# Gathers listed 20 chunks ahead, and steps of six turns whose last adds run in the next step, in a graph layer on one core

## The chip, the cores and the metric

The kernel runs on one core of one Trainium2 chip. Its time is the device time of one execution in microseconds (us). The kernel before took 1976.42 us, the median of three runs (1966.72, 1976.42 and 1977.36).

## The reference

One layer of a message-passing network with residual and layer norm. There are N = 12500 nodes with 128 features each and E = 400000 edges, sorted by their destination `dst`; `src` and the type (0 or 1) of an edge are random. All matrices are 128 x 128.

```python
msg = where(edge_type == 0, x[src] @ W_data.T + b_data, x[src] @ W_ctrl.T + b_ctrl)
agg = segment_sum(msg, dst, num_segments=12500)
out = layernorm(x + relu(agg + x @ W_self.T + b_self))      # over the 128 features, no scale, no shift
```

Since the sum over edges is linear, the kernel sums the rows `x[src]` for each node and type first (and counts the edges for the biases), and multiplies by the weights after. So most of the work is fetching 400000 rows of x by index and adding them up by destination.

## The kernel before

**Data.** x is split at the start into three bf16 parts whose sum is the float32 value (`split_x`, lines 229 to 269). The parts are kept in SBUF as `x3` and stored to DRAM as the table `rows3`, 768 bytes a row. Splitting uses ScalarE (lines 246 and 248) and VectorE (247 and 249); x arrives in eight pieces through ScalarE's DMA queue (line 241), at most four of them in SBUF at a time, and `store` (253) writes the table through SP's queue.

**Two ways to fetch a row.** The edges lie in 3125 chunks of 128, and these in 25 groups of 125. A group is cut into four windows, and each window into a "p" part of 12, 11, 11 or 11 chunks and an "e" part of 20 chunks. So there are 100 windows ("pairs" in the code).

* A **p** chunk is gathered: GpSimd issues one indirect DMA (line 700) that brings 128 rows of `rows3` into a tile `msg`. TensorE multiplies the three parts with a 0/1 matrix `psel` (line 658, three matmuls) that adds each row to the column of its destination, and a fourth matmul with `one_col` counts (712). There are 1125 such chunks.
* An **e** part is fetched from SBUF by TensorE. VectorE sorts its 2560 edges into slots, by the block of x that they read (`give_slots`, lines 505 to 637): 100 blocks, 32 slots each. A matrix `pick` of zeros and ones then selects rows of `x3` (line 732, 98 matmuls, "picks", each 32 x 384, four beside one another in the array) into the PSUM tile `got`. ScalarE copies `got`, two groups of rows at a time, to `emsg` in SBUF (line 743), and TensorE adds the rows up by destination with `esel` (658; VectorE makes `esel` from the slots' codes in three selections, line 463) and counts (761). Edges that find no slot, up to 64 a window, are "spares": their rows come by one more indirect DMA into `last` (line 747).

**A step.** The main loop takes one window w per step (`picked`, lines 718 to 797). The window's 25 groups of rows q are worked on in turns of four: turn t = 0 to 5 picks the rows q = 4t to 4t+3 (`rows`), counts and adds those of the turn before, and a seventh unit, t = 6, adds the last ones, turns the codes and calls `accumulate`, which adds the PSUM tile `sums` into the SBUF accumulator `acc` (line 688). `got` has two buffers in PSUM, `sums` two (shared by the p and the e part), the tile `rk` one.

Beside the picks of w, a step does these things for other windows: the p chunks of a window two steps back (`gathered`, 690 to 716, spread over steps by the lines after `chunks, closed, rest`); the slots of w+2 in the order `before` (TensorE, lines 537 and 479), `ranks` and `rank_matrix` (VectorE, 547 to 562 and 589, the latter makes `rv`), `put` (TensorE, 601, 20 matmuls into `rk`), `spread` (ScalarE copies `cell`, two DMAs on SP's queue write it to DRAM and read it back to all partitions as `pick`), and `turn_codes` and `keep_codes` (TensorE 621 and 489, ScalarE 631, 496 and 498, VectorE 500); the comparison that makes `pick` of w+1 a 0/1 matrix (643); the first selections for w+3; the preparation of the next group's indices and codes (`prep_e`, `prep_p`); and the finishing of 500 nodes (`finish`: product with the weights, norm, store).

**What sets the order.** `merged` sorts the units of all these lists by a position between 0 and 1 within the step, which gives the order in which the program lists instructions. The framework's scheduler then orders each engine's queue from that list: an instruction listed later may be put ahead of one that, by the scheduler's own estimate, isn't ready yet. Each engine runs its queue strictly in that order; buffers of a pool come round in turn, and an instruction waits for the earlier user of its buffer. The pool `msg` has 24 buffers (`AHEAD`). In the queue of GpSimd as built, a spare-row gather therefore stands between chunk gathers whose use comes some two steps later.

**The first part.** Before the loop: loads of indices (`load_first`, `load`, `near_i`, SP's queue), constants, the weights and biases through ScalarE's queue (274 and 275), the places of all windows (`place`, `near`) and the transposed weights `wT`, then the slots of windows 0 and 1 mixed with the splitting of x, then `bparts` (small DMAs of the biases), `store_rows` and `prep_p(0)`.

A long path at the end of the program (a plain loop over all chunks) runs only if a check finds that the input doesn't fit the windows; it isn't taken here.

## Time and profile before

| | us |
|---|---|
| median of three runs | 1976.42 |
| the profiled execution | 2371.03 |
| its span, first to last instruction | 2369.3 |
| TensorE busy / weight loads busy | 1863.1 / 1364.9 |
| VectorE, ScalarE, GpSimd busy | 1584.0, 1229.7, 1412.5 |
| mean granted TensorE clock | 0.909 of full speed |

The profiled execution is longer than the timed ones; only shares and single durations are taken from it, and the times compared are those of the runs. In the profile, PE is TensorE, PEld its weight loads, DVE VectorE, ACT ScalarE, POOL GpSimd and SP the engine whose queue issues most plain DMAs. A row such as "POOL msg L700 <- PE sums L658" means that the instruction of line 700 on GpSimd that writes `msg` waited for an instruction of TensorE, line 658; the numbers are the total in us, how often, and the longest. In a timeline row the first two numbers are start and duration in us, and the bracket at its end is the idle time before it and what ended it. "issue" is a wait for which the profile shows nothing. The busy share of an engine is a mean over the whole span, so the waits and the order of work around a step's boundary say more than the shares.

### The profile page before, as it was taken

How to read it: one execution, taken by the hardware profiler on the slowest of the kernel's cores; microseconds unless marked ns; L12 is line 12 of the kernel's file. 1: busy time of each engine (PE TensorE's matmuls, PEld its weight loads, DVE VectorE, ACT ScalarE, POOL GpSimd, SP SyncE). 2: the span in 40 equal slices, each digit the busy share in tenths (PEclk: the TensorE clock that was granted, in tenths of full speed). 3: DMA queues.
4: the chain of work that ended last, by engine and by line, in shares of the span. 5: the costliest groups of instructions: out<-in, count | busy, mean ns of one | idle time of the engine just before them, and what ended most of it. 6: DMA issues, size and time to landing. Idle time of an engine off the chain costs nothing.

```text
span 2369.3 us, 70786 instructions
## 1 busy us (share of the span) xinstructions
PE 1863.1 (79%) x28867; PEld 1364.9 (58%) x28867; DVE 1584.0 (67%) x4224; ACT 1229.7 (52%) x2322; POOL 1412.5 (60%) x1243
## 2 busy tenths in 40 slices
PE   0468887887878787888888887888888888887977
PEld 0346665665556565666565565665666665665646
DVE  6747676766666666767676766676667666676753
ACT  3435554555445545545555554555555555545635
POOL 0366665756465565665666665566666665676661
PEclk9879898999889899999999988998989999999979
DMA  7423342333333333333323323333323323233321
GB/s 206 148 80 104 97 107 84 109 91 98 87 96 96 100 100 90 109 97 94 108 85 106 107 86 102 97 98 106 107 83 104 102 88 102 89 101 105 97 87 42
DMA packets 185017, 236.73 MB, mean 100 GB/s; under 512 B 80295, under 2 KB 152282, under 8 KB 184682
## 3 DMA queue, kind: packets, MB, share of 16 engines
q0 software_dynamic: 57200, 115.59, 17.7%
q1 hardware_dynamic: 114418, 109.94, 14.8%
q10 hardware_dynamic: 13064, 6.60, 1.0%
q8 instruction: 228, 3.74, 0.7%
q14 instruction: 107, 0.88, 0.1%
HBM read 215.35 MB, written 16.64 MB: 98 GB/s over the span
## 4 chain that ended last, share of the span: by engine, by line
PE 66%; issue 10%; ACT 10%; DVE 6%; another core or an unknown queue 5%; DMA 1%; SPq 1%; DVEq 0%; ACTq 0%; POOL 0%; POOLq 0%
PE sums L658 32%; PE got L732 22%; ACT emsg L743 9%; PE fin L850 3%; PE rk L601 2%; PE sums L761 2%; PE rk L489 1%; PE sums L712 1%; DVE esel L463 1%; PE rk L537 1%; DVE x L249 1%; PE rk L621 1%; DVE xt L247 0%; PE fin L837 0%
## 5 line engine op out<-in xcount | busy, mean ns | idle before, releaser
L700 POOL DMA_INDIRECT msg<-rows,pidx x1125 | 1290.4, 1147 | 790.3 <-PE sums L658 363.4
L743 ACT CAST emsg<-got 128x768 bf16<-128x768 f32 x1200 | 919.8, 804 | 796.5 <-PE got L732 328.8
L732 PE MATMUL got<-x,pick 128*32 128x384 bf16 x9800 | 659.2, 353 | 238.7 <-ACT emsg L743 145.6
L658 PE MATMUL sums<-esel,emsg 128*128 128x176 bf16 x7200 | 751.3, 255 | 48.6 <-issue 46.0
L658 PEld LDWEIGHTS <-emsg 128*128 128x128 bf16 x7200 | 579.8, 104 | 220.0 <-issue 215.4
L463 DVE TENSOR_TENSOR esel<-code_col,code 128x1408 bf16<-128x1408 bf16 (+1 forms) x300 | 275.0, 917 | 348.9 <-PE sums L658 195.7
L732 PEld LDWEIGHTS <-pick 128*32 128x32 bf16 x9800 | 242.3, 97 | 421.3 <-issue 336.0
L658 PE MATMUL sums<-psel,msg 128*128 128x48 bf16 x3375 | 240.0, 187 | 48.0 <-issue 35.3
L658 PEld LDWEIGHTS <-msg 128*128 128x128 bf16 x3375 | 187.8, 99 | 77.6 <-issue 72.5
L747 POOL DMA_INDIRECT last<-rows,idx x100 | 118.1, 1181 | 139.4 <-DMA pdst<-in_dst_dram 91.4
L712 PE MATMUL sums<-psel,one_col 128*128 128x48 bf16 x1125 | 184.5, 185 | 16.9 <-issue 16.8
L688 DVE TENSOR_TENSOR acc<-acc,sums 128x352 f32 (+1 forms) x200 | 94.0, 470 | 132.5 <-PE sums L658 54.0
L761 PE MATMUL sums<-esel,one_col 128*32 128x176 bf16 x2500 | 168.2, 254 | 16.2 <-issue 14.7
L463 DVE TENSOR_TENSOR O<-cell_col,blk 128x2000 bf16<-128x2000 bf16 x100 | 119.3, 1193 | 55.7 <-PE got L732 27.8
L643 DVE TENSOR_SCALAR pick<-pick,lane_f 128x1600 bf16<-128x1600 bf16 x200 | 125.6, 642 | 14.2 <-DMA pick<-there 13.7
L601 PE MATMUL rk<-rv,O 128*128 128x64 bf16 x2000 | 89.0, 198 | 50.3 <-DVE rv L589 35.0
L761 PEld LDWEIGHTS <-one_col 128*32 128x32 bf16 x2500 | 84.2, 103 | 63.7 <-issue 31.1
L547 DVE TENSOR_REDUCE ahead<-rk 128x100 bf16<-128x500 f32 x100 | 67.5, 675 | 78.7 <-PE got L732 55.7
L712 PEld LDWEIGHTS <-one_col 128*128 128x128 bf16 x1125 | 109.6, 97 | 18.0 <-issue 17.7
L551 DVE TENSOR_TENSOR prod<-O,ahead 128x2000 bf16<-128x2000 bf16 x100 | 119.0, 1190 | 0.0
L601 PEld LDWEIGHTS <-O 128*128 128x128 bf16 x2000 | 73.4, 101 | 67.3 <-issue 54.8
L631 ACT CAST code<-rk 128x50 bf16<-128x50 f32 x100 | 20.3, 203 | 173.8 <-PE got L732 68.0
(170 smaller groups left out, 1998.4 us busy)
## 6 DMA issues: line engine op xcount, KB each, us to landing
pick<-there SPq DMA_DIRECT2D x100, 800.0 KB
msg<-rows,pidx POOLq DMA_INDIRECT x1125
rows<-x SPq DMA_DIRECT2D x6, 1344.0 KB
xs<-in_x_dram SPq DMA_DIRECT2D x99, 62.5 KB
out_dram<-h SPq DMA_DIRECT2D x99, 62.5 KB
xt<-in_x_dram ACTq DMA_DIRECT2D x6, 896.0 KB
psrc<-in_src_dram SPq DMA_DIRECT2D x100, 6.0 KB
pdst<-in_dst_dram SPq DMA_DIRECT2D x100, 6.0 KB
```

The costliest lines, as they stand in the source:

```text
L463: nc.vector.tensor_tensor(sel.rearrange("p n (w t) -> p n w t", t=2), col[:rows].rearrange("p (o w t) -> p o w t", o=1, t=2).to_broadcast( ...
L551: nc.vector.tensor_tensor(prod, s["O"], ahead.rearrange("p (o j) -> p o j", o=1).to_broadcast([P, EC, NCELL]), op=OP.mult)
L601: nc.tensor.matmul(s["rk"][:m, :2 * CAP], s["held"][:, c * NCELL:c * NCELL + m], s["rv"][:, c].rearrange("p v r -> p (v r)"), start=(c == ...
L643: nc.vector.tensor_scalar(t, t, lane_f, None, op0=OP.is_equal)
L658: nc.tensor.matmul(out, msg[:, j * D:(j + 1) * D], sel, start=(start and j == 0), stop=stop, skip_group_check=True)
L688: added.append(nc.vector.tensor_add(win, win, ps[:, :4 * wide].rearrange("p (a w) -> p a w", w=wide)[:, :, :width]))
L700: nc.gpsimd.indirect_dma_start(out=msg, out_offset=None, in_=rows3[:, :], in_offset=bass.IndirectOffsetOnAxis(ap=codes["p", g][0][:, i * P ...
L712: nc.tensor.matmul(cnt, one_col, sel, start=False, stop=(c == n - 1), skip_group_check=True)
L732: nc.tensor.matmul(ps[CAP * a:CAP * (a + 1), :], slots[w]["pick"][:, a * NQ + q, :], x3[:, 4 * q + a - a0].rearrange("p j d -> p (j d)"), ...
L743: nc.scalar.copy(msg, ps[:, :, :3 * D])
L747: nc.gpsimd.indirect_dma_start(out=msg[:OVF, :], out_offset=None, in_=rows3[:, :], in_offset=bass.IndirectOffsetOnAxis(ap=slots[w]["idx"], ...
L761: nc.tensor.matmul(cells_of(s["ps"], EW, 1)[CAP * (q % 4):CAP * (q % 4 + 1), :], one_col[:, :CAP], s["sel"][q], start=(q < 4), stop=(q + 4 ...
```

## The change

* **Gathers.** A list `to_fetch` holds all chunks in order. `fetch()` takes the next one, allocates its `msg` and issues its indirect DMA. Twenty fetches (`AHEAD`) are listed before the main loop; then each chunk of the loop first lists the fetch of the chunk 20 places on and uses the oldest fetched tile. The pool keeps 24 buffers (`HOLD`). One tile holds one chunk (`SB` = 1). `spare_rows` moves from turn 1 to turn 2, and `prep_p` of the next group from the third to the second step of a group, since its indices are read earlier.
* **Joined steps.** `picked` returns six turns and a function `end`. The adds of the last four or five groups of rows, the codes (`turn_codes`, `keep_codes`) and `accumulate` of step w are listed in turn 0 of step w+1, after its first 16 picks and its first selection. After the last step, `ending()` is called once more. The finishing units (`rest`) are spread from 0.1 on.
* **Placing.** `put` and `spread` move from turn 5 to turn 4 of the six.
* **First part.** The first nodes of the p and the e parts have a tile each, so that `node0` reads only the e part's. The weights and biases come through SP's queue. The places, `near` and `wT` are made in `places_and_weights`, listed near the end of the mixed list, and the first piece of x is split before `prep_e(0)`.

The diff, cut to its core:

```diff
-AHEAD = 24
+SB = 1
+HOLD = 24
+AHEAD = 20
...
-    first_i = keep.tile([1, NG, NWIN], I32, name="first_i")
+    first_i = {k: keep.tile([1, NG, NE], I32, name=f"first_{k}") for k in "ep"}
     def load_first(kind):
-        for i, (k, _, c, _) in enumerate(windows(0)):
+        for k, i, c, _ in windows(0):
-                    out=first_i[:, :, i:i + 1],
+                    out=first_i[k][:, :, i:i + 1],
...
     for i, (w, b) in enumerate(zip(ws, bs)):
-        nc.scalar.dma_start(out=wn[:, i, :], in_=w)
-        nc.scalar.dma_start(out=brow[:, i, :], in_=b.rearrange("(o d) -> o d", o=1))
+        nc.sync.dma_start(out=wn[:, i, :], in_=w)
...
-    first = first_i.rearrange("o g w -> o (g w)")
+    first = first_i["e"].rearrange("o g w -> o (g w)")
...
-    near = keep.tile([rows_p, NG], FP, name="near")
...
-    nc.vector.tensor_scalar(near, near_i, from_f, None, op0=OP.add)
...
+    nc.vector.tensor_copy(node0, fin0[:, :NG * NE].rearrange("p (g w) -> p g w", w=NE))
+    def places_and_weights():
+        near = raw["near"] = keep.tile([rows_p, NG], FP, name="near")
...
+        nc.vector.tensor_scalar(near, near_i, from_f, None, op0=OP.add)
+        place = tmp.tile([1, 2, NG, NWIN], FP, name="place")
...
+        for at, k in enumerate("pe"):
+                each = place[:, 0].rearrange("o g (i k) -> o g i k", k=2)[:, :, :, at]
+                nc.vector.tensor_tensor(
+                    each, first_i[k], ref.rearrange("o g (i k) -> o g i k", k=2)[:, :, :, at], op=OP.subtract
+                )
...
+        wps = ps1.tile([P, 512], FP, name="fin")
+        for i in range(3):
+            nc.tensor.transpose(wps[:, i * D:(i + 1) * D], wn[:, i, :], ident)
+        nc.scalar.copy(wT, wps[:, :3 * D].rearrange("p (i d) -> p i d", d=D))
...
-        s["tiled"] = {5: [put, spread], 6: [turn_codes, keep_codes]}
+        s["tiled"] = {4: [put, spread], 6: [turn_codes, keep_codes]}
...
+    to_fetch = [(g, i, c) for g in range(NG) for i in range(NE) for c in range(0, PC[i], SB)]
+    fetched = []
+
+    def fetch():
+        if to_fetch:
+            g, i, c = to_fetch.pop(0)
+            msg = mp.tile([P, SB, 3 * D], BF, name="msg")
+            for k in range(min(SB, PC[i] - c)):
+                at = i * PB + c + k
+                nc.gpsimd.indirect_dma_start(
+                    out=msg[:, k, :], out_offset=None, in_=rows3[:, :],
+                    in_offset=bass.IndirectOffsetOnAxis(ap=codes["p", g][0][:, at:at + 1], axis=0),
+                )
+            fetched.append(msg)
...
         def chunk(c):
-            msg = mp.tile([P, 3 * D], BF, name="msg")
-            nc.gpsimd.indirect_dma_start(
-                out=msg, out_offset=None, in_=rows3[:, :],
-                in_offset=bass.IndirectOffsetOnAxis(ap=codes["p", g][0][:, i * PB + c:i * PB + c + 1], axis=0),
-            )
+            if c % SB == 0:
+                fetch()
+                s["msg"] = fetched.pop(0)
...
-            add_rows(rows, msg, sel, c == 0, c == n - 1)
+            add_rows(rows, s["msg"][:, c % SB, :], sel, c == 0, c == n - 1)
...
-    def picked(w, tiled):
+    def picked(w, tiled, ending):
...
+        def add(q0, q1):
+            for q in range(q0, q1):
+                add_rows(cells_of(s["ps"], EW, 0), s["msg"].pop(q), s["sel"][q], False, q == NQ - 1)
+
         def unit(t):
-            if t < turns:
-                for q in range(t * per, (t + 1) * per, pair):
-                    rows(q)
+            for q in range(t * per, (t + 1) * per, pair):
+                rows(q)
+            if t in (0, 1):
+                choose(8 * t)
             if t == 0:
-                choose(0)
-            if t == 1:
-                choose(8)
+                ending()
+            if t == 2:
                 spare_rows()
             if t == 3:
                 choose(16, 9)
-            if 0 < t < turns:
+            if t > 0:
                 for q in range((t - 1) * per, t * per if t < turns - 1 else NQ):
                     count(q)
-            if t < turns:
-                for u in tiled.get(t, []):
-                    u()
+            for u in tiled.get(t, []):
+                u()
             if t == turns - 1:
                 last_rows()
             if t > 0:
-                for q in range((t - 1) * per, t * per if t < turns else NQ):
-                    add_rows(cells_of(s["ps"], EW, 0), s["msg"].pop(q), s["sel"][q], False, q == NQ - 1)
-            if t == turns:
-                for u in tiled.get(t, []):
-                    u()
-                accumulate(g, 2 * i + 1, s["ps"], EW, EW)
+                add((t - 1) * per, t * per)
+
+        def end():
+
+            add((turns - 1) * per, NQ)
+            for u in tiled.get(turns, []):
+                u()
+            accumulate(g, 2 * i + 1, s["ps"], EW, EW)
         turns = (NQ - 1) // per
-        return evenly([lambda t=t: unit(t) for t in range(turns + 1)])
+        return evenly([lambda t=t: unit(t) for t in range(turns)]), end
...
+    split_units.pop(0)()
     prep_e(0)
-    merged(evenly(all_slots(0) + all_slots(1)), evenly(split_units))
+    merged([(0.97, places_and_weights)], evenly(all_slots(0) + all_slots(1)), evenly(split_units))
...
-    mp = ctx.enter_context(tc.tile_pool(name="msg", bufs=AHEAD))
+    mp = ctx.enter_context(tc.tile_pool(name="msg", bufs=HOLD))
...
+    for _ in range(AHEAD):
+        fetch()
...
+    def ending():
+        pass
...
-        if i == 2 and g + 1 < NG:
+        if i == 1 and g + 1 < NG:
             more += evenly(prep_p(g + 1), 0.1, 0.7)
...
+        units, ending = picked(w, tiled, ending)
         merged(
             chunks.pop(w, []),
-            picked(w, tiled),
+            units,
             begin,
             pick_matrix(w + 1) if w + 1 < pairs else [],
             more,
-            evenly(rest),
+            evenly(rest, 0.1),
...
+    ending()
     for u in rest:
         u()
```

## The prediction

> **What bounds the kernel now.** I read the share lines of the page, then the chain of waits, then who waited for whom on TensorE and on GpSimd, then the timeline of one step boundary and of the prologue.
>
> ```profile
> PE 1863.1 (79%) x28867; PEld 1364.9 (58%) x28867; DVE 1584.0 (67%) x4224; ACT 1229.7 (52%) x2322; POOL 1412.5 (60%) x1243
> PE 66%; issue 10%; ACT 10%; DVE 6%; another core or an unknown queue 5%; DMA 1%; SPq 1%; DVEq 0%; ACTq 0%; POOL 0%; POOLq 0%
> ```
>
> TensorE is the longest busy engine and carries 66% of the chain; ScalarE, which empties the PSUM tile "got" for it, carries 10%. GpSimd, which issues the gathers, is 60% busy and 0% of the chain.
>
> ```profile
> PE got L732 <- ACT emsg L743: 145.6, 192, 8.4
> PE sums L658 <- issue: 87.1, 186, 4.6
> PE rk L601 <- DVE rv L589: 35.0, 2, 19.8
> PE rk L537 <- ACT part L498: 20.8, 33, 1.1
> PE sums L658 <- DVE acc L688: 7.3, 11, 2.1
> PE sums L658 <- DMA msg<-rows,pidx: 2.1, 3, 1.2
> ...
> POOL msg L700 <- PE sums L658: 363.4, 278, 11.2
> ```
>
> The first figure is the total. TensorE's largest named wait is for ScalarE to free "got"; it waited 2.1 us in all for gathers. GpSimd waits 363.4 us for TensorE to give buffers back: the gathers are ahead. Counting gathers finished against chunks consumed in the timeline, the lead is 20 to 24 chunks at 95% of the 1125 uses.
>
> ```profile
> 1018.40 0.39 PE L658 MATMUL sums<-esel,last 128*128 128x176 bf16 x3
> 1018.73 0.20 PE L621 MATMUL rk<-ident_b,cell 128*32 128x25 bf16 x4
> ...
> 1019.38 0.83 PE L732 MATMUL got<-x,pick 128*32 128x384 bf16 x16
> ...
> 1020.93 0.40 PE L537 MATMUL rk<-prod,ltri 128*128 128x125 bf16 x4 [0.52 <-ACT part L498]
> ...
> 1021.63 0.51 PE L732 MATMUL got<-x,pick 128*32 128x384 bf16 x8 [0.18 <-ACT emsg L743]
> ```
>
> This is a boundary between steps. The old step's adds are finished, so between the first 16 picks and the next 8 TensorE has only gathered chunks to do, and waits twice for ScalarE. Adding up every idle bracket of TensorE over 92 steps (200 to 2280 us, mean step 22.7 us) by the number of picks done since the boundary, the waits for ScalarE's copies of "got" are 0.26 us a step after 16 picks, 0.07 after 24, 0.41 after 32, 0.21 after 40: 0.95 together, of 4.0 us idle a step.
>
> **The sum's base.** The profiled execution took 2371.03 us (span 2369.3); the median of the runs shown is 1976.42, 0.834 of it. I sum in profiled microseconds and multiply by 0.834; unscaled, the answer would move by 6 us.
>
> **Gathers 20 ahead.** In the old order as built, the scheduler already puts a chunk's gather some 24 chunks before its use, so listing it 20 ahead changes the place of the spare-row gathers among them and little else. It can gain at most the 2.1 us above. It could lose if the lead fell: 20 chunks are 1.7 steps, 39 us, against 1.45 us for a gather and its gap (1147 ns mean plus the 0.30 issue gap). I take 0. The spare-row gather moves from turn 1 to turn 2, but its rows are now used in the next step's first turn; four turns cover it. The work of prep_p one step earlier is the same work, and evenly(rest, 0.1) shifts the finishing parts by a tenth of a step: 0 for both, hidden under TensorE; uncovered, prep_p is some 1.5 us on VectorE in 24 groups.
>
> **Joined steps.** The last turn's adds (12, the 3 on "last"), the codes and the accumulate now stand behind the next step's first 16 picks. I weighed the matmuls of both built orders at the timeline's pace (52 ns a pick from 16 in 0.83; 85 an add, between 76 in a dense run, 12 in 1.08, and the page's mean of 104; 21 to 36 for the small ones). TensorE work other than picks, between pick groups, is:
> after 16 picks: 0.66 us before, 1.87 after; after 32: 1.21 and 1.32; after 80: 1.75 and 1.92; before the two last picks: 0.95 and 0.38; between those and the next step's first picks: 3.03 and 1.09.
> ScalarE needs 1.50 us for two copies (its rows "x2"). So the wait behind 16 and 24 picks goes, and with ScalarE's backlog most of that behind 32 and 40: -0.80 of the 0.95 (bounds -0.3, the first two alone, and -0.95). New is the tight end of the step: the two last picks need the first of two buffers back, with 0.42 (8 picks) + 0.38 of cover for 0.80 of copy plus 0.2 of hand-over, and then the small copy (0.47) stands in ScalarE's queue before the next picks: +0.25 (0 to +0.7). The matmuls of "before" (line 537) wait for the code copies of the one "rk" bank; the work between falls from 1.43 to 0.99 and the three copies take 0.31 plus hand-over: +0.10 (0 to +0.4). The next step's first count needs a "sums" bank; from the last add to it the work falls from 2.28 to 1.72 (shortest 0.99), and the accumulate needs 0.52, unless VectorE is inside a 1.2 us selection: +0.05 (0 to +0.3).
>
> **Placing in the fifth turn.** "put" (20 matmuls, 0.78 us) needs VectorE's rv. TensorE's work from line 537 to put falls from 11.18 to 9.27 at that pace; a step's real interval is 16.7 us, so put comes 2.85 us earlier. In 92 steps put started a median 3.2 us after rv was done; shifting each by 2.85 gives a mean wait of 0.32. But the third selection of codes, on which VectorE waits for TensorE, stands four operations (1.6 us of rows) later in the new VectorE order, so rv itself should come about 1 us earlier; a shift of 1.9 gives 0.08. I take +0.10 (0 to +1.3, the latter at a shift of 4.5). The DMAs of put (there, pick) issue earlier on SP; pick is used more than half a step later, and all waits for it now come to 13.7 us on VectorE: 0, and a gain of those 13.7 at most if they were on the path.
>
> The step's sum is -0.80 + 0.25 + 0.10 + 0.05 + 0.10 = -0.30 us, 100 times: **-30 us**.
>
> **New first part.** ScalarE's own DMA queue now holds only x; before, its six weight and bias issues ended at 23.5 us, and its first cast of x began at 26.21. VectorE's first subtraction was at 28.33. With the first nodes in two tiles, its first work of 18.06 no longer waits for both kinds of load. The new VectorE order still has the places (21.3) and the load of psrc (22.4) ahead, so it starts near 24: -4 us (0, if x's later pieces bind as at 56.44, where ScalarE waited 5.56 for one; -10). The weights' issues take 2.2 us of SP, ahead of loads for the second group and of stores that can't start before 38: 0. The 20 gathers stand before the first two spare-row gathers, which so land some 25 us later (20 x 1.25). Their adds stand at the end of step 1 in TensorE's new order.
>
> ```profile
> 96.07 3.27 POOL L747 DMA_INDIRECT last<-rows,idx  x1 [91.39 <-DMA pdst<-in_dst_dram]
> ```
>
> ```profile
> 100.00:110.00 10.00, 6.29 (x58) 3.48 (x59) 2.73 (x5) 1.50 (x2) 7.56 (x9) 0.69 0.41 94
> 110.00:120.00 10.00, 0.83 (x8) 0.28 (x8) 5.80 (x16) 1.78 (x3) 7.87 (x8) 0.65 0.25 70
> 120.00:130.00 10.00, 3.67 (x24) 1.60 (x24) 0.00 (x0) 0.95 (x2) 7.56 (x9) 0.50 0.29 78
> ```
>
> (Columns: stretch, its length, busy us and instructions of PE, PEld, DVE, ACT and POOL, granted clock, DMA share, GB/s.) While GpSimd issued the first 26 gathers (96 to 132 us) TensorE did almost nothing (0.83 us busy in one stretch of 10, clock down to 0.50), and step 1 ended at 142. In the new order the spares land near 92 + 25 + 5 = 122, before that: -3 (0 to -17). The first part gives **-7 us**.
>
> Sum: -37 profiled us, times 0.834 is -31: **1945 us**.
>
> The Trainium skill (Perfetto Trace Analysis, Identifying the Most-Contended Engine) says to judge VectorE, ScalarE and GpSimd by busy share, TensorE by weight-load share, and to relieve the highest. By it the bound is VectorE (67% against 58%), from which this change takes nothing: 1976. The chain above, with DVE at 6% and PE at 66%, speaks for the sum instead. The skill's TensorE: Matmul & The Clock Gate (Part 1) lets the clock fall after about 3.4 us of idleness; the removed waits are shorter, so by it no clock is won, and I add none. The trace agrees as far as it goes: 0.50 stands where TensorE waited 4 to 8 us at a time.
>
> **Rivals.**
> *The wait only moves* (same): if the end of the step takes +0.7 in place of +0.25, the step gives +0.15 and all that is left is the first part: 1983; at +0.55 it gives 0 and 1970. Taken in the middle: 1976. For it: ScalarE has 12 copies a step, 9.6 us, and the gap at the end is really tight. Against it: ScalarE is 52% busy and idles 257.0 us behind TensorE's adds.
> *VectorE becomes the bound at put* (slower): TensorE's order is fixed, so put waiting for rv holds all behind it. If rv gains nothing and put moves 3.5 us, the mean wait is 0.64 a step: +24 - 7 = +17, 1990. At 4.5 us it is 1.28: +88 - 7 = +81, 2044. It decides from a wait of 0.5 us a step. For it: the unprofiled step is shorter while VectorE's 15.8 us of work isn't. Against it: both steady-state waits for rv in the trace are none (the two above, 35.0 us, lie in the prologue).
> *Bursts go too* (faster): inside runs of six or more gathers TensorE is idle 23% of the time, outside 13 to 18%, over 682 us; if even spacing removes it, some 55 us more: 1899. For it: the prologue's windows. Against it: the cause of the idleness isn't shown.
>
> **How the numbers follow.** Forecast 0.50 (own range from 1910, half way to all its terms' good bounds, -122 profiled us or 1875, up to 1966), bursts 0.10, only moves 0.18, VectorE 0.22. A half per cent, 10 us, is about what this measurement can tell. Faster is 0.50 + 0.10 = 0.60, less 0.01 for the forecast's upper edge; same 0.17: that 0.01, 0.15 of "only moves" and 0.01 of the VectorE case; slower 0.24: the rest of both. The range reaches from half way into the bursts' case, 1890, to the milder half of VectorE's, 2005.
>
> **What would show it.** Right: TensorE's wait for emsg well under 145.6 and few such brackets behind the first 16 picks; GpSimd's lead unchanged; picks starting before 74 us. Wrong: a new row "PE rk <- DVE rv" of tens of us in the steady state, or waits for emsg before the last two picks; TensorE waiting for msg or last.

## The result, and the profile after

The changed kernel takes **2032.65 us** (median of 4 runs, 2022.16 to 2038.86) where the kernel before takes 1971.57 (4 runs, 1946.87 to 1977.36): a ratio of **1.038, 95% interval 1.026 to 1.050**. It is slower, and 2033 lies above the forecast of 1945 and above its range, which ended at 2005.

To read these numbers one thing must be known: the runs fall in two kinds by the chip that they ran on, for in the recorded times and on one chip of the experiments (the "first kind" below) the kernel before takes 1972 and 1980 us, on four others (the "second kind") 2381 to 2424 us, and the profile that the prediction was read from (2371 us) has the rows of the second kind. Every ratio below is against the kernel before on the same chip.

The profile of the changed kernel (2038.86 us, span 2037.2) is of the first kind. Its page, share lines, chain, and the line of the gathers (after the bar: busy us, mean ns of one; then idle time ahead of them):

```profile
PE 1720.8 (84%) x28867; PEld 1298.5 (64%) x28867; DVE 1566.0 (77%) x4225; ACT 1219.5 (60%) x2322; POOL 1537.8 (75%) x1243
...
PE 42%; DVE 25%; DMA 18%; issue 6%; POOL 4%; ACT 3%; DVEq 1%; SPq 0%; POOLq 0%; ACTq 0%
...
L707 POOL DMA_INDIRECT msg<-rows,pidx x1125 | 1420.8, 1263 | 432.6 <-issue 157.3
```

The waits of the changed kernel (who waited for what: us in all, times, longest):

```profile
PE sums L665 <- DMA last<-rows,idx: 176.9, 51, 19.7
PE rk L608 <- DVE rv L596: 46.3, 50, 12.0
PE got L754 <- ACT emsg L765: 24.1, 76, 1.6
...
POOL msg L707 <- issue: 157.3, 516, 0.3
POOL msg L707 <- DVE pcode L415: 90.0, 1, 90.0
POOL msg L707 <- PE got L754: 62.2, 204, 0.3
POOL msg L707 <- PE sums L665: 54.0, 177, 0.3
POOL msg L707 <- DMA msg<-rows,pidx: 36.0, 118, 0.3
```

The rows of GpSimd (POOL) carry the result. Apart from the first start, no wait of its msg gathers is longer than 0.3 us, whoever is named as the releaser: 0.30 us is simply the gap between one gather and the next. One gather of spare rows waits 10.7 us for TensorE; otherwise GpSimd never stands still. From its first gather at 94.66 us to the end of the last at 2011.9 it issues 1225 gathers (1125 msg, 100 last) at a pitch of 1.565 us, 1.252 for a mean gather and 0.313 for a mean gap. So 94.7 + 1225 x 1.565 = 2012, and 25 us of finishing make the span. It is "75% busy" and still the engine that sets the end. TensorE shows it from its side: its one large wait is for the spare rows ("last"), which stand in GpSimd's queue among the msg gathers. The wait for "emsg", around which the prediction was built, is 24.1 us.

What did the old kernel look like on the same kind of chip? The first experiment shows it.

### The profile page after: what moved, and what is told of

Read it like the earlier page. It is cut to its first block, busy times and chain, and to the rows that moved or that the text cites. A ratio compares the mean times of both kernels' runs of the same rounds, so it can differ in the third digit from the quotient of the medians.

```text
span 2037.2 us, 70698 instructions
## 1 busy us (share of the span) xinstructions
PE 1720.8 (84%) x28867; PEld 1298.5 (64%) x28867; DVE 1566.0 (77%) x4225; ACT 1219.5 (60%) x2322; POOL 1537.8 (75%) x1243
## 4 chain that ended last, share of the span: by engine, by line
PE 42%; DVE 25%; DMA 18%; issue 6%; POOL 4%; ACT 3%; DVEq 1%; SPq 0%; POOLq 0%; ACTq 0%
PE sums L665 18%; PE got L754 13%; DMA last<-rows,idx 9%; DMA msg<-rows,pidx 6%; POOL msg L707 4%; DVE esel L470 3%; PE fin L877 3%; PE rk L608 2%; DVE rv L596 2%; DVE prod L558 2%; DVE pick L650 2%; ACT emsg L765 2%; PE rk L544 2%; DVE found L567 2%; PE rk L496 1%
## 5 line engine op out<-in xcount | busy, mean ns | idle before, releaser
L707 POOL DMA_INDIRECT msg<-rows,pidx x1125 | 1420.8, 1263 | 432.6 <-issue 157.3
L665 PE MATMUL sums<-esel,emsg 128*128 128x176 bf16 x7200 | 702.2, 246 | 0.0
L665 PEld LDWEIGHTS <-emsg 128*128 128x128 bf16 x7200 | 546.6, 100 | 170.0 <-issue 158.2
L754 PE MATMUL got<-x,pick 128*32 128x384 bf16 x9800 | 633.9, 344 | 24.7 <-ACT emsg L765 24.1
L754 PEld LDWEIGHTS <-pick 128*32 128x32 bf16 x9800 | 231.3, 97 | 144.3 <-issue 39.9
L695 DVE TENSOR_TENSOR acc<-acc,sums 128x352 f32 (+2 forms) x200 | 93.7, 469 | 277.5 <-PE sums L665 249.4
L665 PE MATMUL sums<-psel,msg 128*128 128x48 bf16 x3375 | 214.9, 187 | 2.0 <-DVE acc L695 1.3
L665 PE MATMUL sums<-esel,last 128*128 128x176 bf16 x300 | 44.9, 266 | 176.9 <-DMA last<-rows,idx 176.9
L665 PEld LDWEIGHTS <-last 128*128 128x128 bf16 x300 | 24.0, 104 | 187.9 <-DMA last<-rows,idx 187.7
L608 PE MATMUL rk<-rv,O 128*128 128x64 bf16 x2000 | 78.1, 195 | 46.7 <-DVE rv L596 46.3
```

The source lines that it names most:

```text
L608: nc.tensor.matmul(s["rk"][:m, :2 * CAP], s["held"][:, c * NCELL:c * NCELL + m], s["rv"][:, c].rearrange("p v r -> p (v r)"), start=(c == ...
L665: nc.tensor.matmul(out, msg[:, j * D:(j + 1) * D], sel, start=(start and j == 0), stop=stop, skip_group_check=True)
L695: added.append(nc.vector.tensor_add(win, win, ps[:, :4 * wide].rearrange("p (a w) -> p a w", w=wide)[:, :, :width]))
L707: nc.gpsimd.indirect_dma_start(out=msg[:, k, :], out_offset=None, in_=rows3[:, :], in_offset=bass.IndirectOffsetOnAxis(ap=codes["p", g][0] ...
L754: nc.tensor.matmul(ps[CAP * a:CAP * (a + 1), :], slots[w]["pick"][:, a * NQ + q, :], x3[:, 4 * q + a - a0].rearrange("p j d -> p (j d)"), ...
```

## Experiments on a chip of the first kind

**The kernel before, once more.** No edit.

> The kernel before, unchanged, for a second profile of it. In its first profile TensorE stood idle for 190 us of 'issue' and GpSimd ran 24 chunks ahead; that execution took 2371 us against 1972 of the timed ones, so it may not show what bounds the timed ones. Theory A (GpSimd's gathers bound the changed kernel only because of their order): a profile near 1970 us in which GpSimd still has real waits for TensorE's buffers, well over the 0.30 us between two gathers. Theory B (the pace of the gathers bounds both kernels): GpSimd runs without a break here too, from about 96 us to about 1945, at (1945 - 96) / 1225 = 1.51 us a gather against 1.56 in the changed kernel.

Measured: 1985.64 us; 13 runs of the same kernel beside it had a median of 1980.03 (1972.54 to 1992.43). Its page and waits:

```profile
PE 1671.7 (84%) x28867; PEld 1274.0 (64%) x28867; DVE 1569.5 (79%) x4224; ACT 1214.0 (61%) x2322; POOL 1486.9 (75%) x1243
...
PE 41%; DVE 26%; DMA 19%; issue 5%; POOL 3%; ACT 2%; DVEq 1%; SPq 1%; POOLq 0%; ACTq 0%
...
L700 POOL DMA_INDIRECT msg<-rows,pidx x1125 | 1364.3, 1213 | 342.9 <-issue 137.8
```

```profile
PE sums L658 <- DMA last<-rows,idx: 181.2, 54, 15.0
PE rk L601 <- DVE rv L589: 46.6, 12, 19.8
...
PE got L732 <- ACT emsg L743: 7.9, 21, 1.4
...
POOL msg L700 <- issue: 137.8, 452, 0.3
POOL msg L700 <- PE got L732: 83.8, 275, 0.3
POOL msg L700 <- PE sums L658: 53.6, 176, 0.3
```

The old kernel is bound in the same way: every gap of GpSimd is 0.3 us but one of 6.6, and TensorE waits 7.9 us for "emsg" in the whole run, not 145.6. The joined steps had nothing to win here. The difference of the two kernels is in the gathers, taken from the two timelines:

| | first gather starts | last ends | mean gather | mean gap | gathers of 3 us or more |
|---|---|---|---|---|---|
| before | 95.31 | 1957.5 | 1.211 | 0.310 | 6 |
| changed | 94.66 | 2011.9 | 1.252 | 0.313 | 52 |

1225 gathers that are 0.042 us longer make 51 us, and the one long wait (10.7 instead of 6.6 us) makes 4 more; the last gather ends 54 us later, and the span is 53 us longer. What has to be explained is the 0.042 us.

**Is it the order of the gathers?** The kernel before with the gathers 20 ahead (the list, a pool of 24, and prep_p one step earlier), and the changed kernel with none ahead:

```
-                msg = mp.tile([P, 3 * D], BF, name="msg")      (kernel before)
-                nc.gpsimd.indirect_dma_start(...)
+                fetch(); msg = fetched.pop(0)                  (and 20 fetch() ahead)
```
```
-AHEAD = 20                                                     (changed kernel)
+AHEAD = 0
```

> Before, with only the gathers listed 20 chunks ahead (and the next group's indices one step earlier). Theory A (the spare-row gathers queued among chunk gathers that are not urgent hold TensorE up): most of the loss, a ratio of 1.02 to 1.04, and TensorE waiting for the spare rows as in the changed kernel (176.9 us). Theory B (the order of the gathers is indifferent, their pace counts): 0.99 to 1.01. My forecast had put this part at 0.

> The changed kernel with the chunk gathers listed at their use again (none listed before the loop, 24 buffers); joined steps, placing and first part stay. Theory A: the loss goes, 0.97 to 1.00, the 37 profiled us of my forecast for the other parts give 0.98. Theory B: it stays at 1.02 to 1.04, because what stretched the gathers is in the joined steps.

Measured: 1995.46 us for the first, 1.005 (1.002 to 1.008) of the kernel before; 2039.29 for the second, 1.024 (1.016 to 1.032). The long gathers stay where they were: 6 of 3 us or more in the first (mean of msg 1218 ns), 53 in the second (1273 ns). The order of the gathers is worth about half a per cent in the first (0.8 at the end of its interval), and without it the second still takes 2039 us, where the whole change took 2033 on the chip of the recorded times. So the loss is in the other parts of the change.

**Where the long gathers lie.** In the changed kernel's timeline nearly all of them cover the same piece of VectorE's program. VectorE and then GpSimd around one (start, us, engine, line, operation):

```profile
251.53 0.17 DVE L569 CAST rank<-found 128x40 bf16<-128x40 f32 x1
251.62 0.97 DVE L470 TENSOR_TENSOR esel<-code_col,code 128x1584 bf16<-128x1584 bf16 x1
252.51 0.48 DVE L470 TENSOR_TENSOR rm<-rank_col,rank 128x640 bf16<-128x640 bf16 x1
252.92 0.36 DVE L531 TENSOR_TENSOR eq<-eq,tri 128x400 bf16<-128x400 bf16 x1
253.19 0.48 DVE L596 TENSOR_TENSOR rv<-rm,node 128x640 bf16<-128x640 bf16 x1
253.60 0.48 DVE L596 TENSOR_TENSOR rv<-rm,code 128x640 bf16<-128x640 bf16 x1
```

```profile
251.86 3.02 POOL L769 DMA_INDIRECT last<-rows,idx  x1 [0.30 <-DVE rank L569]
255.19 0.99 POOL L707 DMA_INDIRECT msg<-rows,pidx  x1 [0.30 <-PE rk L608]
```

The gather starts inside the third selection (esel, 128x1584) and ends 0.80 us after the last rv; an undisturbed gather takes 0.95 us in all. Of the 52 gathers of 2.9 us or more, 49 contain the end of an rv, and they end a median 0.82 us after it. It looks as if a gather that begins in this run of operations does no work until the run is over. In the old kernel's order the small cast "rank" stood mostly between esel and the run, with eq, rm, eq, rv, rv behind it: 1.84 us from the first eq's start to the second rv's end in a step near 1002 us. The new order puts rank ahead of esel, so that esel joins the run (in 66 of 100 steps, against 8 in the old kernel): 2.46 us from its start to the second rv's end in the rows above. Between 200 and 1930 us, 52 gathers of the changed kernel begin 1.75 to 2.25 us ahead of the end of the second rv, and take a mean 2.79 us; in the old one 20 do, and take 1.64.

This run is not the only place. Of the 329 gathers of the changed kernel that take 1.3 to 4.5 us, 313 end 0.80 to 0.87 us after the end of some operation of VectorE, mostly a tensor_tensor (chance would give some 46); in the old kernel 300 of 327 do. So gathers stand behind VectorE in both kernels: together they take 319 us more than 0.95 us each in the old one and 370 in the changed one. The gathers that end behind an rv have 55 us of this before and 91 after. Those that end behind the 500-column `prod` (line 530 before, 537 after) have 1 and 35; that `prod` comes directly behind another tensor_tensor, the last "half", in 44 steps before and 86 after, since the reduction "found" (line 560 before, 567 after) stood between them in 48 of the old steps and in 10 of the new. All the others together fall by 19.

The Trainium skill bears on this (SBUF — State Buffer, "SBUF: two separate sides" and "Who interferes with whom"): VectorE and GpSimd share a pair of SBUF ports under an exclusive lock, held for a whole instruction, and a gather issued from GpSimd can be held up by VectorE because its descriptors can't be written meanwhile. This case agrees in kind. The page infers that a tensor_tensor does not stop the writing of descriptors, but also says that one with two inputs in SBUF contends with a GpSimd instruction that reads SBUF; a gather's row indices (`pidx`, `idx`) lie in SBUF, so the page leaves open on which side it falls. The measurement decides: here the operations beside the 3 us gathers are tensor_tensors with two inputs in SBUF, and in this kernel a run of them goes with a gather that stands. It gives about 115 ns from the end of VectorE's operation to the end of the wait; the trace shows only the end of the gather, 0.82 us after the last operation.

That the run is the cause, and that it is the whole loss, had to be tested. All further experiments met chips of the second kind. There TensorE also stands for no visible reason, and GpSimd has real waits for it, so that two questions come apart: what the change gives TensorE, and what it costs GpSimd.

## Experiments on chips of the second kind

**The changed kernel itself.** No edit.

> The changed kernel as it is, beside the kernel before on the same chip. If GpSimd sets the end there (every gap between gathers 0.30 us, as in the profiles of 1985 and 2039 us): 1.025-1.05 of the kernel before and over 30 gathers of 3 us. If TensorE sets the end there (waits of TensorE on 'issue' of 200 us in all and waits of GpSimd for TensorE over 300 us, as in the profile that the prediction was read from): faster than the kernel before, 0.96-0.99, as the prediction's sum had it.

Measured: 2347.56 us against 2381.16, **0.986 (0.979 to 0.993)**: on this chip the change is faster by 33.6 us. The prediction's sum in its own profiled microseconds was -37. The page and the waits of this run:

```profile
PE 1865.3 (79%) x28867; PEld 1366.9 (58%) x28867; DVE 1566.8 (67%) x4225; ACT 1229.5 (52%) x2322; POOL 1492.0 (64%) x1243
...
PE 68%; issue 8%; ACT 8%; DVE 7%; another core or an unknown queue 5%; POOL 1%; DMA 1%; DVEq 0%; ACTq 0%; SPq 0%
```

```profile
PE got L754 <- ACT emsg L765: 116.3, 138, 5.7
PE got L754 <- issue: 68.1, 118, 5.3
PE sums L665 <- issue: 60.3, 123, 1.9
PE rk L544 <- ACT part L505: 52.1, 38, 7.3
...
POOL msg L707 <- PE sums L665: 271.4, 220, 10.1
```

These are like the rows that the prediction started from: TensorE in 68% of the chain, and GpSimd waiting 271.4 us, up to 10.1 at a time, for TensorE. The long gathers are here too (35), but GpSimd has waits that can hide them: its gaps ahead of gathers beyond the fixed 0.30 us sum to some 370 us here, against 16 us in the profile of 2039 us.

**The place of put.** The changed kernel with put and spread back in the sixth turn, run on two chips:

```
-        s["tiled"] = {4: [put, spread], 6: [turn_codes, keep_codes]}
+        s["tiled"] = {5: [put, spread], 6: [turn_codes, keep_codes]}
```

> The changed kernel with put and spread back in the sixth turn; all else as changed. The run esel, rm, eq, rv, rv stays in VectorE's order in most steps. Theory C: as the changed kernel, 2010-2045 us, over 30 gathers of 3 us and more. Rival P (placing in the fifth turn is what costs, because TensorE then stands for rv): back to 1975-1995 us with PE rk<-DVE rv under 25 us.

> The changed kernel with put and spread back in the sixth turn. Theory C: within 15 us of the changed kernel on the same chip, since esel, rm, eq, rv, rv stay in one run, over 30 gathers of 3 us and more. Rival P (placing in the fifth turn costs, TensorE stands for rv there): 25-60 us below the changed kernel.

Measured: 2411.11 us, 0.998 (0.994 to 1.002) of the kernel before, and 2373.47 us, 1.000 (0.997 to 1.004), the latter on the chip on which the whole change gave 0.986. The long gathers stay (30 and 38), as theory C had it. The time is not what either theory expected: 26 us above the changed kernel. So with put in the sixth turn the joined steps, the first part and the gathers ahead give nothing between them, although the wait that the joined steps were to remove did shrink. In the waits of the second of these runs:

```profile
PE got L754 <- issue: 94.4, 150, 4.1
PE got L754 <- ACT emsg L765: 75.9, 93, 5.3
```

The wait for "emsg" was 145.6 us in the profile that the prediction was read from, on another run of the second kind, and is 84.9 on the other chip here. What took its place is not shown. TensorE's busy time is 1885.0 us, against 1865.3 with put in the fifth turn on the same chip, and its waits on "issue" sum to 232 us against 170. A wait that moves with put is VectorE's for the buffer of O, which put gives back: 60 us in all with put in the fifth turn, 163 us in the sixth. In the kernel before, with put late as well, it is 54 us, so the 163 seem to belong to joined steps and a late put together, and the 26 us can't be put down to either alone. That this wait is the 26 us is not shown.

**The run broken.** The changed kernel with the third selection listed one turn earlier, so that VectorE does it between the half additions:

```
             if t == 2:
                 spare_rows()
-            if t == 3:
                 choose(16, 9)
```

> The changed kernel with the third selection of a step (esel, 128x1584) listed in the third turn and not in the fourth, so that on VectorE it stands between the two half additions and not directly ahead of rm, eq, rv, rv. Theory C (GpSimd's gathers are back to back in both kernels and set the end; the change lengthens them because esel now joins rm, eq, rv and rv to one unbroken run of VectorE operations with two inputs in SBUF, and a gather that begins in it stands until its end): the gathers of 3 us and more go from 47 to under 10, the mean msg gather from 1263 ns to 1210-1225 ns, the time from 2033 to 1975-2000 us (0.999 to 1.015 of the kernel before). Rival D (the joined steps cost by themselves, in whatever order VectorE works): still over 30 gathers of 3 us and 2020-2045 us.

> The changed kernel with the third selection (esel, 128x1584) listed in the third turn. Theory C: where GpSimd sets the end, gathers of 3 us and more go from over 30 to under 10, the mean msg gather from about 1260 to 1210-1225 ns, and the time falls 35-60 us below the changed kernel on the same chip. Rival D (the joined steps lengthen the gathers in any order of VectorE): within 15 us of the changed kernel, over 30 long gathers.

Measured: 2334.70 us, 0.963 (0.956 to 0.970), and 2294.45 us, 0.965 (0.959 to 0.970), the latter 53 us below the changed kernel on the same chip. Gathers of 3 us or more: 10 and 11, against 30 with put in the sixth turn on the first of these chips and 35 in the changed kernel on the second. The gathers of the changed kernel and of this one, on the same chip:

```profile
L707 POOL DMA_INDIRECT msg<-rows,pidx x1125 | 1371.7, 1219 | 779.6 <-PE sums L665 271.4 <-issue 182.9 <-PE got L754 128.8
```

```profile
L707 POOL DMA_INDIRECT msg<-rows,pidx x1125 | 1287.5, 1144 | 795.4 <-PE sums L665 279.7 <-issue 176.7 <-PE got L754 154.4
```

One selection moved takes 75 ns off the mean gather; esel stands in the run in none of the 100 steps, and no gather stands behind the 500-column `prod` any more. Rival D, that the joined steps lengthen the gathers in any order, falls here. The time falls too, although GpSimd is not the bound all the time. Part of that is not the gathers' doing: TensorE's own busy time falls from 1865.3 to 1834.9 us, with the granted clock at 0.945 instead of 0.914.

**Is GpSimd the bound when it has more to do?** One memset of 1x8 elements on GpSimd, listed behind each of the 1125 gathers of the kernel before:

```
             nc.gpsimd.indirect_dma_start(out=msg, ...)
+            nc.gpsimd.memset(more_pool, 0.0)
```

> The kernel before with a memset of 1x8 elements on GpSimd behind each of the 1125 msg gathers; all else as before. Theory C (GpSimd sets the end): the time grows by 1125 times what the memset takes on GpSimd with its gap, which the trace will show; an estimate from the 0.30 us gap between gathers is 0.1 to 0.4 us each, +110 to +450 us. Rival T (TensorE sets the end and GpSimd has 20% to spare): less than +20 us.

Measured: 2436.97 us, 1.021 (1.016 to 1.026), +56 us. In the queue as built, the memsets don't stand behind their gathers. Nothing else uses their tile, and the scheduler puts them early: 651 run before the first gather, which so starts at 110 us and not at 95, and the other 474 in bunches that end at 321 us. From there on it is the kernel before. So the run does not show what a longer GpSimd costs throughout, and decides nothing; the next edit puts in more.

**GpSimd made the bound for part of the run.** Five such memsets a gather, in the kernel before, in the changed one, and in the one with the run broken, on one chip:

```
             nc.gpsimd.indirect_dma_start(out=msg, ...)
+            [nc.gpsimd.memset(more_pool, 0.0) for _ in range(5)]
```

> The kernel before with five memsets of 1x8 on GpSimd for each of the 1125 msg gathers (0.104 us each with about 0.055 us between, by the run with one memset: some 0.8 us a gather, 895 us in all). Theory C: GpSimd sets the end on either kind of chip; the time is about 120 + 1225 x 1.45 + 895 = 2790 us, 2700-2900. Rival T (there is room on GpSimd on every chip): below 2500 us.

> The changed kernel with the same five memsets for each msg gather. Theory C: with GpSimd the bound, nothing of what the joined steps give TensorE is left, and the lengthened gathers cost 10 to 60 us: 1.003-1.02 of the kernel before with the same memsets. If the joined steps helped in themselves whatever the bound: 0.98-0.99 of it.

> The changed kernel with the third selection in the third turn and the same five memsets for each msg gather. Theory C: 10 to 60 us below the changed kernel with the memsets, level within 0.7% with the kernel before with the memsets. Rival D: as the changed kernel with the memsets.

Measured: 2974.18 us (2960.74 to 2985.63), 3021.83 (3015.23 to 3031.89) and 2972.11 (2958.84 to 2981.01). The gathers of the three, in that order:

```profile
L701 POOL DMA_INDIRECT msg<-rows,pidx x1125 | 1227.0, 1091 | 692.2 <-issue 272.6
```

```profile
L708 POOL DMA_INDIRECT msg<-rows,pidx x1125 | 1320.6, 1174 | 661.2 <-issue 286.6
```

```profile
L708 POOL DMA_INDIRECT msg<-rows,pidx x1125 | 1249.5, 1111 | 680.6 <-issue 263.0
```

Of 3 us or more are 1, 22 and 3 gathers. By the times alone the change costs 48 us (1.016), and moving the one selection gives all of it back (0.999 of the kernel before). But these memsets come early too. The first and the last bunch of them in the first of the three runs, each with the gather behind it:

```profile
4.65 104.04 POOL L705 MEMSET more_pool<- 1x8 bf16 x651
109.66 1.08 POOL L749 DMA_INDIRECT last<-rows,idx  x1 [0.97 <-issue]
...
1858.93 1.31 POOL L705 MEMSET more_pool<- 1x8 bf16 x9
1860.85 0.95 POOL L701 DMA_INDIRECT msg<-rows,pidx  x1 [0.61 <-issue]
```

So each run has two stages. Up to its last memset GpSimd sets the pace: beyond its fixed gaps (0.30 us behind a gather, 0.61 behind a bunch) it waits 16 to 17 us in all, and TensorE waits 746 to 834 us for the spare rows ("last"). Behind it GpSimd waits 220 to 260 us again, and TensorE only 8 to 10 us for "last". The stages from the three timelines, one profile each, in us:

| | last memset ends at | gathers until then | they take | from there to the last gather's end |
|---|---|---|---|---|
| before | 1860.2 | 646 | 672.6 | 1087.4 |
| changed | 1926.9 | 647 | 739.6 | 1078.0 |
| changed, run broken | 1890.1 | 647 | 703.3 | 1063.8 |

With GpSimd the bound, time follows the gathers one for one: the change lengthens them by 67 us and the stage by 67, and moving the one selection takes 36 us off the gathers and 37 off the stage. That is about half of the cost. The other 31 us stay with the selection moved, so in this stage rival D is half right; which of the other changes of order makes them is not shown. They are made up behind the last memset, where GpSimd is not the bound and the two new orders are 9 and 24 us faster than the old. The expectation of 2700 to 2900 us for the first run left out that second stage: it took GpSimd for the bound to the end.

**Half of the gathers left out**, in the kernel before and, by the like edit of its list (10 fetches of two chunks each ahead), in the changed one, so that every second chunk adds the rows of the chunk ahead of it:

```
-            msg = mp.tile([P, 3 * D], BF, name="msg")
-            nc.gpsimd.indirect_dma_start(out=msg, ...)
+            if c % 2 == 0:
+                s["msg"] = mp.tile([P, 3 * D], BF, name="msg")
+                nc.gpsimd.indirect_dma_start(out=s["msg"], ...)
+            msg = s["msg"]
```

> The kernel before with 525 of its 1125 msg gathers left out: every second chunk multiplies the rows of the chunk ahead of it, so the output is not the reference's. All else stays. Theory C (GpSimd sets the end): the gathers need 725 x about 1.5 = 1090 us and no longer bind, so the time falls from 1980 to the next limit, 1780-1900 us (VectorE and TensorE are busy 1570 and 1672 us). Rival T (TensorE sets the end, as the prediction had it): 1950-1985 us.

> The changed kernel with the same 525 msg gathers left out (fetched 20 chunks ahead as before). Theory C: it too falls below 1900 us, and with GpSimd out of the way what the joined steps save on TensorE shows for the first time: 20-70 us below the kernel before with the same gathers left out, if the prediction's 0.3 to 0.7 us a step were right; above or level with it, if that part was wrong by itself. Rival T: 2010-2045 us.

Measured: 2129.29 us (0.878) and 2005.68 us (0.827), the second 124 us, 5.8%, below the first. With GpSimd at 40 and 46% the changed kernel's program is clearly the better one for the other engines, by more than the 102 us (122 profiled) that all good bounds of the prediction came to. But 2129 us is far above the 1780 to 1900 expected, and it is lower than 2418 by 289 us although GpSimd had been waiting for TensorE there: on these chips fewer gathers also make TensorE faster. Why is not known. It is not chiefly its waits on "issue", in which it stands for nothing that the profile shows: they sum to 201 us here and to 219 in the profile of 2371 us, while TensorE's busy time is 1752.3 against 1863.1 us. Those waits do set the second kind of chip apart: 68.1 and 60.3 us in the rows of the changed kernel above, none among the rows of its waits in the profile of 2039 us.

**A better version?** The kernel with the run broken was run three more times, on one of the chips above and on two others, and once with the gathers at their use as well:

> The changed kernel with the third selection in the third turn. Where GpSimd sets the end (kernel before near 1980 us), theory C: 0.995-1.015 of the kernel before and under 15 gathers of 3 us; rival D (the joined steps cost there by themselves): 1.025-1.05. Where TensorE sets the end (kernel before near 2390 us): 0.96-0.97 as in the two runs of it so far.

> The changed kernel with the third selection in the third turn, once more, for a chip on which the kernel before takes about 1980 us. There, theory C: 0.995-1.015 of the kernel before and under 15 gathers of 3 us; rival D: 1.025-1.05. On a chip where the kernel before takes about 2400 us: 0.96-0.97.

> The same with the gathers listed at their use (none ahead). By the pair of runs on the order of gathers: within 0.7% of the run beside it on either kind of chip.

> The changed kernel with the third selection in the third turn. Where the kernel before takes about 1980 us, theory C: 0.995-1.015 of it, under 15 gathers of 3 us, mean msg gather 1210-1225 ns; rival D: 1.025-1.05. Where the kernel before takes about 2400 us: 0.96-0.97.

Measured: 0.968 (0.962 to 0.974), 0.966 (0.959 to 0.974), with gathers at their use 0.967 (0.960 to 0.974), and 0.966 (0.961 to 0.972). All were chips of the second kind, where the kernel before took 2418 to 2424 us. There this version beats both kernels: the kernel before by 3.2 to 3.7%, the changed one by 2.3% (2294.45 against 2347.56). On a chip of the first kind, where the recorded comparison was made, it has not been run. The stage in which the memsets made GpSimd the bound suggests that it would lie between the two kernels there, with about half of the loss left; that is an estimate.

## Why the prediction was wrong

The step that failed is "What bounds the kernel now": TensorE as the longest busy engine with 66% of the chain, "GpSimd, which issues the gathers, is 60% busy and 0% of the chain", "the gathers are ahead". That was true of the profiled execution of 2371 us and false of the executions that were timed. The step "The sum's base" carried it over: it saw that the profiled execution was 1.2 times the median of the runs and multiplied the sum by 0.834, as if every engine shrank alike. The prediction's own rows showed that one could not: 1225 gathers of 1147 ns with a 0.30 us gap are 1773 us; with the 96 us ahead of the first and some 25 behind the last that is 1894 of the 1976. An engine with no more than 4% to spare is not off the path. What would fill a run that is 395 us shorter was asked of VectorE alone, in the rival on put, and not of GpSimd.

By its steps:

- **Joined steps, -0.80 of "got" waits, -0.40 with what they bring.** On the first kind the waits that were to go hardly existed (7.9 us in the run, and 24.1 after the change). On the second kind (one profile each) they fell from 145.6 to 116.3 us with the whole change, 0.3 a step, and to 75.9 and 84.9 with put in the sixth turn, 0.6 to 0.7 a step. The wait behind "before" grew from 20.8 to 52.1 us, 0.31 a step, with the whole change and to 36.5 and 26.5 with put in the sixth turn, where +0.10 was priced. So with put late these terms were about right as waits, and the time still did not fall (0.998 and 1.000): the step that fails there is that a wait removed is time won.
- **Placing in the fifth turn, +0.10.** Wrong in sign on the second kind, together with the joined steps: 26 us between two runs on one chip, some 0.3 us a step. On the first kind it was not tried alone. The rival that put would wait for rv named 1990 to 2044 us, and the measured time lies in it, but by luck: the wait did not grow (46.3 us in all, 46.6 in the kernel before, though in 50 waits instead of 12).
- **Gathers 20 ahead, 0.** About right: +0.5% on the first kind, and nothing on the second (2338 and 2340 us with the run broken).
- **New first part, -7.** The picks start at 71.1 us, before the 74 that was named, against 76.7. It is hidden: the gathers set the end, and the first of them starts 0.65 us earlier.
- **The rows that move in VectorE's order.** The prediction saw that the third selection stood four operations later in the new order and priced that for TensorE alone. Its cost is to GpSimd, by way of the gathers, and no rival named it. Longer gathers are 51 of the 53 us. How much of them is this one selection is not settled, since moving it back was not run on the first kind: where GpSimd was the bound for a stage, it gave back 36 of 67 us.

The sum of -37 us met -33.6 on a chip of the kind whose rows it was made from. That is luck: the terms that it counted on gave nothing without the placing, which it had counted as a cost.

## What to carry to other kernels

When the profiled execution is much longer than the timed ones, don't scale the sum: take each engine's work with its fixed gaps, see which would fill the shorter time, and make the sum for that engine too. An engine whose every gap between instructions is the same short figure has no slack, whatever its busy share says. And when a change reorders VectorE, look at which operations become neighbours: GpSimd's gathers paid here for an unbroken run of operations with two inputs in SBUF. When an instruction is added as a load, look in the trace where it stands before reading its price: 651 of 1125 memsets that were listed behind gathers ran before the first gather.

## What the runs showed of the hardware

- A gather on GpSimd takes 0.95 us by itself and up to 3.0 us, seldom more, when it begins in a run of tensor_tensors that have both inputs in SBUF; it ends some 0.82 us after the run does, and 313 of the 329 gathers of 1.3 to 4.5 us in the changed kernel end within 0.80 to 0.87 us of an operation of VectorE. That the shared port is the reason is the reading that fits; it was not isolated.
- The same program takes 1972 us in the recorded comparison, 1980 on one chip of the experiments, and 2381 to 2424 us on four others. No chip was seen in both kinds, so whether it is the chip or its condition at the time is not shown. On the latter TensorE has waits on "issue" of up to 5 us, spread over the run (219 us in the profile of 2371 us, none in that of 1985), and its busy time is longer for the same 28867 matmuls, 1863.1 against 1671.7 us at a granted clock of 0.909 against 0.939. The gathers' transfers don't differ: the software queue's packets filled 21.3% of 1984 us and 17.7% of 2369 us, 423 and 419 us. What slows TensorE there stays open, and so does why leaving out 525 gathers takes 289 us off there.
- The sign of a change can turn with the kind of chip: 0.986 on a chip of the second kind, 1.038 in the recorded comparison, and neither interval reaches 1.
